# Softmax maxima by 32x32 block transposes and one TensorE transpose, in a two-layer cross-attention kernel

## Chip, cores and metric

The kernel runs on one core of a Trainium2 chip. The metric is the device time of one execution in microseconds (us); where several executions were timed, their median is used. All arithmetic is float32. The engines are TensorE (PE; its weight loads are shown apart as PEld), VectorE (DVE), ScalarE (ACT), GpSimd (POOL) and SyncE (SP, which issues most DMAs).

## What is computed

Two cross-attention layers, one after the other, on x of 4 batches x 512 tokens x 320 channels, with a context of 4 x 1024 tokens x 512. There are 20 heads of 16 channels. The last 4 context tokens are "ip" tokens in layer 0; in layer 1 the first 77 are text and all others ip. Cut to what matters (`heads` splits the channels):

```python
# layer 0
q, k_t, v_t = heads(x @ W_q), heads(text @ W_k), heads(text @ W_v)
probs_t = softmax(q . k_t * 0.25)                 # over 1020 text tokens
text_out = probs_t @ v_t
attn_scores = q . heads(ip @ W_k_ip) * 0.25       # 4 ip tokens
qsem = l2norm(probs_t @ text);  sem = qsem . l2norm(ip)
probs_ip = softmax(attn_scores + 0.5 * sem) * spatial_mask
x = (text_out + probs_ip @ heads(ip @ W_v_ip)) @ W_out + b_out + x
# layer 1
out = softmax(q . k * 0.25) @ v                   # over 77 text tokens
    + softmax(q . k_ip * 0.25) @ v_ip             # over 947 ip tokens
x = out @ Wo.T + bo + x
```

Each softmax subtracts the maximum over its own tokens, per query and head.

## The kernel before, in words

**Tiling.** The queries come in 16 turns: 4 batches of 4 tiles of 128 tokens (`TURNS`, line 34). A turn has 5 groups of 4 heads (`HG`), so there are 80 groups of layer 0 (`G`, line 491) and 80 of layer 1. Layer 1 of a turn can begin when layer 0 of that turn is finished, so its groups run beside the layer-0 groups of later turns: 75 of them as objects of class `Once` (line 557), the last turn's 5 by another routine (`twice`, line 696).

**Scores.** `fill` (line 510) makes the scores of one group for half of the context tokens. Four heads lie in four 32-row strips of the `kq` and `qq` tiles, 16 rows used in each. Scores have the context tokens on the partitions and (head, token block, query) along the free axis: two PSUM tiles `sc` of 128x1024. ScalarE copies each to SBUF (`e`, line 523), VectorE reduces each over the token blocks into `m` (line 525); after the second half the two halves of `m` are combined (line 528).

**Maxima.** What is left is a maximum over 128 partitions, for 4 heads x 128 queries. TensorE transposes `m` head by head (four transposes of 128x128, `max0`, line 835; in layer 1 another four of the first token block, where text and ip meet, `maxima`, line 572). VectorE reduces the transposes out of PSUM into `zz` (four or eight columns, line 847 and lines 584 to 587), turns `zz` by one 32x32 block transpose and SyncE writes it to DRAM in four DMAs (`spread`, line 531). Broadcast DMAs bring it back to all partitions as `bc`. VectorE adds `bc` to `e`, and ScalarE takes the exponential in place (lines 597 to 604 for layer 1, 854 to 863 for layer 0; GpSimd subtracts one head's exponentials from the other's at line 865).

**The ip tokens of layer 0** are the last four partitions of the last token block. Lines 824 to 826 put `drop` (-1e30 on these partitions) into `m`, line 861 puts it into the exponent, and lines 828 to 830 copy the four score rows to a tile `ips`, which `finish` transposes at line 1023.

**Products of layer 0.** A group has two units (class `Unit`, line 903) of two heads. A unit has seven products of eight matmul records each, in four parts: `11`, `12` (part 0), `t1` and `s2`x`t2` (part 1), `22` and `t3` (part 2), `t4` (part 3). Their results lie in two PSUM banks, and VectorE or ScalarE must read a bank (`c`, `p`, `u`, `pv` in the trace) before it is written anew; `t1` writes the bank that product `12` used, so it waits for `c` and `pv` of part 0. GpSimd adds into `e` between products (lines 933, 952, 955).

**Values of layer 1.** `add_values` (line 538) multiplies the exponentials with the values into `pv`; ScalarE copies it to `pc`. In `normalise` (line 657) VectorE spreads the denominators over 32 partitions by a shuffle and takes their reciprocal over 128x256; GpSimd multiplies and adds text and ip. `project` (line 668) multiplies the five groups with `wo1`.

**Order.** All instructions of TensorE, and those of VectorE that go through `vec`, keep the order of the program (lines 76 to 92). The order is written out by hand: after each part k = 0 to 7 of a group (4 per unit), `stop` (line 1155) runs one step of waiting work. Even stops `visit`: the fills of the next layer-0 group at k = 0 and 2, those of a layer-1 group at k = 4 and 6, the `pv` products of the one before at 6. Odd stops take steps of finishing a turn (`after`, `late`) and of the projections (`proj`) of the next batch, which are used up in the first 12 or so of a batch's 20 groups; the last batch has none to prepare. Exponentials follow at k = 1 and 6 (layer 0, `ew`), 3 and 5 (layer 1, `do_adds`), `normalise` at 1 (at 5 in a turn's first group). The transposes of the maxima stand in part 0, between products `11` and `12` (line 953): of layer 1 in a group's first unit, of layer 0 in its second. Behind the last group the remaining work of layer 1 follows in a loop (line 1215).

## Time and profile before

| | us |
|---|---|
| median of 3 runs | 3419.3 (3416.9 to 3419.7) |
| the profiled execution | 3412.7 |
| its span, first to last instruction | 3411.0 |
| TensorE busy | 3302.7 |
| VectorE busy | 2486.3 |
| ScalarE busy | 1787.4 |
| GpSimd busy | 1036.4 |
| transposes `mx` of the maxima, 920 | 141.4 |
| reductions `zz` out of PSUM, 305 | 168.0 |
| shuffle and reciprocal of layer 1's denominators, 80 each | 175.3 |

The profile is of one execution. Busy time of an engine is the time in which at least one of its instructions runs; matmuls overlap, so the time between the starts of two of them says more than a record's duration. A float32 product stands as two records, a transpose as one. In the timeline each line has start, duration, engine, line of the program (L77 is the helper for matmuls, L92 that for transposes, L87 that for VectorE), the operation, out<-in by the program's names, and in brackets how long the engine was idle before and what ended that.

### The profile page before, as it was taken

How to read it: one execution, taken by the hardware profiler on the slowest of the kernel's cores; microseconds unless marked ns; L12 is line 12 of the kernel's file. 1: busy time of each engine (PE TensorE's matmuls, PEld its weight loads, DVE VectorE, ACT ScalarE, POOL GpSimd, SP SyncE). 2: the span in 40 equal slices, each digit the busy share in tenths (PEclk: the TensorE clock that was granted, in tenths of full speed). 3: DMA queues.
4: the chain of work that ended last, by engine and by line, in shares of the span. 5: the costliest groups of instructions: out<-in, count | busy, mean ns of one | idle time of the engine just before them, and what ended most of it. 6: DMA issues, size and time to landing. Idle time of an engine off the chain costs nothing.

```text
span 3411.0 us, 74812 instructions
## 1 busy us (share of the span) xinstructions
PE 3302.7 (97%) x28417; PEld 2666.0 (78%) x28417; DVE 2486.3 (73%) x4300; ACT 1787.4 (52%) x3220; POOL 1036.4 (30%) x1066
## 2 busy tenths in 40 slices
PE   7999999999999999999999999999999999999978
PEld 6777887878778888887878788787877878787855
DVE  2344676688877766788886776778888888888864
ACT  1344455555555555555555555556555655565642
POOL 2323223233233222333333222223333333333220
PEclk9999999999999999999999999999999999999986
DMA  7423444333434444332345444332242332232221
GB/s 211 103 58 99 103 112 102 91 67 66 102 93 118 101 110 120 69 67 57 71 97 131 103 100 110 88 71 60 63 100 65 64 61 64 58 67 60 59 52 34
DMA packets 644271, 292.23 MB, mean 86 GB/s; under 512 B 491162, under 2 KB 598394, under 8 KB 643914
## 3 DMA queue, kind: packets, MB, share of 16 engines
q1 hardware_dynamic: 642874, 283.83, 35.1%
q8 instruction: 228, 3.74, 0.5%
q0 software_dynamic: 864, 3.41, 0.4%
q14 instruction: 129, 1.06, 0.1%
q10 hardware_dynamic: 176, 0.20, 0.0%
HBM read 245.95 MB, written 40.63 MB: 84 GB/s over the span
## 4 chain that ended last, share of the span: by engine, by line
PE 83%; DVE 10%; DMA 2%; ACT 2%; issue 2%; SPq 1%; POOL 0%; DVEq 0%; POOLq 0%; ACTq 0%
PE b L77 53%; PE sc L77 9%; PE pt_k L77 4%; PE pv L77 4%; PE pt_v L77 4%; DVE e L87 4%; PE mx L92 3%; DVE m L87 2%; PE pt_q L77 2%; PE pt_y L77 1%; DVE den L87 1%; ACT e L523 1%; PE ex L77 1%; PE mx L77 1%; ACT e L604 1%
## 5 line engine op out<-in xcount | busy, mean ns | idle before, releaser
L87 DVE TENSOR_REDUCE m<-sc 128x256 f32<-128x1024 f32 (+1 forms) x620 | 662.2, 1084 | 163.6 <-PE sc L77 119.8
L87 DVE TENSOR_TENSOR e<-e,bc 128x768 f32<-128x768 f32 (+2 forms) x770 | 751.4, 1024 | 14.0 <-DMA bc<-zd 14.0
L77 PE MATMUL b<-xv_t,e 128*128 128x277 f32 x2560 | 685.2, 409 | 21.8 <-DVE pv L87 15.0
L77 PE MATMUL b<-xv,e 128*128 128x277 f32 x2560 | 652.7, 397 | 8.6 <-ACT e L863 8.6
L523 ACT COPY e<-sc 128x1024 f32<-128x1024 f32 x620 | 613.2, 1009 | 70.0 <-DVE m L87 39.3
L77 PEld LDWEIGHTS b<-xv_t,e 128*128 128x128 f32 x2560 | 460.3, 189 | 150.1 <-issue 10.3
L77 PEld LDWEIGHTS b<-xv,e 128*128 128x128 f32 x2560 | 470.3, 190 | 111.5 <-ACT e L863 10.7
L865 POOL TENSOR_TENSOR e<-e 128x512 f32<-128x512 f32 x160 | 206.8, 1292 | 1059.0 <-ACT e L863 1059.0
L937 ACT ACTIVATE junk<-c 128x256 f32<-128x256 f32 x480 | 198.6, 414 | 523.5 <-DVE c L87 520.5
L604 ACT ACTIVATE e<-e 128x1024 f32<-128x1024 f32 x300 | 312.5, 1057 | 238.5 <-DVE e L87 232.8
L952 POOL TENSOR_TENSOR e<-e,s 128x512 f32<-128x512 f32 x160 | 211.8, 1324 | 578.6 <-PE b L77 554.4
L77 PEld LDWEIGHTS sc<-qq,kq 16*128 16x128 f32 x9920 | 306.2, 186 | 102.3 <-issue 96.2
L863 ACT ACTIVATE e<-e 128x1024 f32<-128x1024 f32 x320 | 337.4, 1057 | 59.3 <-DVE e L87 50.0
L77 PE MATMUL sc<-qq,kq 16*128 16x128 f32 x9920 | 365.7, 283 | 2.0 <-DMA kq<-kd 1.1
L87 DVE TENSOR_TENSOR c<-b,p 128x256 f32<-128x256 f32 x320 | 134.5, 420 | 312.3 <-PE b L77 303.8
L77 PE MATMUL b<-xs,e 128*128 128x256 f32 x1280 | 304.6, 381 | 0.0
L77 PE MATMUL b<-xs_t,s 128*128 128x256 f32 x1280 | 302.9, 379 | 0.0
L77 PE MATMUL b<-xs_t,e 128*128 128x256 f32 x1280 | 302.4, 379 | 0.0
L77 PEld LDWEIGHTS b<-xs_t,s 128*128 128x128 f32 x1280 | 243.3, 190 | 39.7
L77 PEld LDWEIGHTS b<-xs_t,e 128*128 128x128 f32 x1280 | 243.2, 190 | 33.1
L77 PEld LDWEIGHTS b<-xs,e 128*128 128x128 f32 x1280 | 239.2, 190 | 36.3 <-issue 2.0
L955 POOL TENSOR_TENSOR e<-e,s 128x512 f32<-128x512 f32 x160 | 206.3, 1290 | 186.1 <-PE b L77 185.8
(201 smaller groups left out, 3634.3 us busy)
## 6 DMA issues: line engine op xcount, KB each, us to landing
kq<-kd SPq DMA_DIRECT2D x632, 64.0 KB
bc<-zd SPq DMA_DIRECT2D x155, 256.0 KB
v1q<-v1d SPq DMA_DIRECT2D x80, 373.5 KB
xv<-v0d SPq DMA_DIRECT2D x320, 42.0 KB
xv_t<-v0d SPq DMA_DIRECT2D x320, 42.0 KB
bc<-zd SPq DMA_DIRECT2D x75, 154.0 KB
L_xattn_W_k<-in_L_xattn_W_k_dram SPq DMA_DIRECT2D x13, 640.0 KB
L_xattn_Wv_ip<-in_L_xattn_Wv_ip_dram SPq DMA_DIRECT2D x13, 640.0 KB
```

Of the source, the lines that this page charges most:

```text
L77: tc.keep_in_program_order(nc.tensor.matmul(out, lhsT=lhsT, rhs=rhs, start=start, stop=stop, skip_group_check=on))
L87: return lambda *args, **kw: keep(getattr(self.engine, name)(*args, **kw))
L92: tc.keep_in_program_order(nc.tensor.transpose(out, in_, ident))
L523: nc.scalar.copy(e[i].rearrange("p h t s -> p (h t s)"), ps[i].rearrange("p h n -> p (h n)"))
L604: nc.scalar.activation(flat, flat, AF.Exp)
L863: nc.scalar.activation(flat, flat, AF.Exp)
L865: nc.gpsimd.tensor_tensor(e[:, 1], e[:, 1], e[:, 0], ALU.subtract)
L937: nc.scalar.activation(junk, x, AF.Square, accum_out=self.w["ss"][:, self.h + r, k : k + 1])
L952: nc.gpsimd.tensor_tensor(self.e("11"), self.e("11"), self.s2, ALU.add)
L955: nc.gpsimd.tensor_tensor(self.e("12"), self.e("12"), self.s2, ALU.subtract)
```

## The change

The maxima are first folded on VectorE: a block transpose turns every 32x32 block of the 128x512 maxima, a reduction over the inner 32 leaves 16 columns (4 heads x 4 blocks of queries) per softmax in `zz`, and one TensorE transpose of `zz` brings the four partition blocks side by side; a last reduction on VectorE takes the maximum over these four, with the sign turned. `spread` writes that in one DMA. In layer 1, which has two softmaxes, ScalarE adds a mask column (`cut`) to the first token block when the first half is filled, and the fold has two block transposes, two additions with the other mask column, and a reduction of both at once. The folds stand at the stops k = 3 (layer 0) and 7 (layer 1), and the transposes move behind product `12`.

The ip mask of layer 0 becomes a 17th row of keys (-1e30 on the last four tokens) against a 17th row of ones in the queries, so that the scores come out masked, the second half's reduction runs over all four blocks, and `drop` goes. The ip scores, which the masked scores no longer hold, are computed in `finish` from the queries and the ip keys (`kip`, spread by heads with a mask `ownk`).

In layer 1's `normalise`, a block transpose of `pc` puts the denominators into one column, so that the reciprocal has 8 numbers per partition; pairs of groups are packed and turned back by a block transpose (`turn_back`), and the projection has three products for five.

```diff
-    zz = [cst.tile([P, ZW], F32, name=f"zz{l}") for l in range(2)]
+    zz = cst.tile([P, P], F32, name="zz")
...
+    nc.vector.memset(qq[0][0], 1.0)
+    nc.vector.memset(kq[0][0], 0.0)
+    for r in range(4):
+        rows = kq[0][0][32 * r : 32 * r + 32, T - NIP :]
+        nc.gpsimd.affine_select(out=rows, in_=rows, compare_op=ALU.not_equal, fill=NEVER, base=-D,
+                                pattern=[[0, NIP]], channel_multiplier=1)
...
+                kip = st2.tile([P, NC, NIP], F32, tag="kip", name=f"kip_{b}")
+                nc.gpsimd.memset(kip, 0.0)
+                for c, (c0, m) in enumerate(CK):
+                    nc.sync.dma_start(kip[:m, c, :], z.kd[0][c0 : c0 + m, T - NIP :])
+                z.kip = st2.tile([P, NC, H, NIP], F32, tag="kipd", name=f"kipd_{b}")
+                nc.gpsimd.tensor_tensor(z.kip, kip.unsqueeze(2).to_broadcast([P, NC, H, NIP]), ownk, ALU.mult)
...
+        n = D + 1 - l
...
-        lo, hi = (1 - c, TH) if l else (0, TH - c)
+        lo = l * (1 - c)
...
-                              ps[j][:, :, lo * P : hi * P].rearrange("p h (t s) -> p h s t", s=P), AX.X, ALU.max)
+                              ps[j][:, :, lo * P : TH * P].rearrange("p h (t s) -> p h s t", s=P), AX.X, ALU.max)
         if c:
-            vec.tensor_tensor(m[:, 0], m[:, 0], m[:, 1], ALU.max)
+            vec.tensor_tensor(m[:, l], m[:, 0], m[:, 1], ALU.max)
+        elif l:
+            for i in range(2):
+                nc.scalar.activation(m[:, 2, 2 * i : 2 * i + 2, :], e[i][:, :, 0, :], AF.Identity, bias=cut[:, 0:1])
...
+    def blocks(m, o, i):
+        vec.transpose(m[:, o].rearrange("p h s -> p (h s)"), m[:, i].rearrange("p h s -> p (h s)"))
+
+    def turn_tops(name):
+        pt = tp(f"mx{name}")
+        tr(pt[:, 0:P], zz, ident)
+        return pt
+
+    def spread(pt, rows, tag, name):
+        n = rows * P // ZW
+        zt = st2.tile([ZW, ZW], F32, tag="zt", name=f"zt{name}")
+        vec.tensor_reduce(zt[:n, :], pt[:n, 0:P].rearrange("r (b j) -> r j b", j=ZW), AX.X, ALU.max, negate=True)
         zd = dr.tile([rows, P], F32, tag=tag, name=f"{tag}{name}")
-        for k in range(P // ZW):
-            nc.sync.dma_start(zd[:, ZW * k : ZW * (k + 1)], zt[ZW * k : ZW * k + rows, :])
+        nc.sync.dma_start(zd.rearrange("h (k j) -> (h k) j", j=ZW), zt[:n, :])
...
+        def fold(self):
+            m = self.m
+            self.folded = True
+            blocks(m, 0, 2)
+            for i in range(2):
+                x = m[:, 1, 2 * i : 2 * i + 2, :]
+                vec.scalar_tensor_tensor(x, self.e[0][i][:, :, 0, :], cut[:, 1:2], x, ALU.add, ALU.max)
+            blocks(m, 2, 1)
+            vec.tensor_reduce(zz[:, 0:ZW].rearrange("p (w r) -> p w r", w=2),
+                              m[:, 0:3:2].rearrange("p w h (k j) -> p w (h k) j", j=ZW), AX.X, ALU.max)
...
-            d = big.tile([P, 2 * P], F32, tag="den", name=f"den1_{turn}_{g}")
-            vec.stream_shuffle(d, pc, [D] * 32)
-            vec.reciprocal(d, d)
-            nc.gpsimd.tensor_tensor(d, pc, d, ALU.mult)
-            nc.gpsimd.tensor_tensor(box["o"][:, g, :], d[:, 0:P], d[:, P:], ALU.add)
+            d = big.tile([P, 8, ZW], F32, tag="den", name=f"den1_{turn}_{g}")
+            r = big.tile([P, 8], F32, tag="rden", name=f"rden1_{turn}_{g}")
+            vec.transpose(d.rearrange("p k w -> p (k w)"), pc)
+            vec.reciprocal(r, d[:, :, D])
+            if g % 2 == 0:
+                if g:
+                    turn_back(g // 2 - 1)
...
+            lo = D * (g % 2)
+            nc.gpsimd.tensor_tensor(d[:, :, 0:D], d[:, :, 0:D], r.unsqueeze(2).to_broadcast([P, 8, D]), ALU.mult)
+            nc.gpsimd.tensor_tensor(box["t"][:, :, lo : lo + D], d[:, 0:4, 0:D], d[:, 4:8, 0:D], ALU.add)
...
-            for g in range(HG):
-                mm(pt[:, 0:C], box["o"][:, g, :], wo1[:, g, :], g == 0, g == HG - 1)
+            for n in range(NO):
+                mm(pt[:, 0:C], box["o"][:, n, :], wo1[:, n, :], n == 0, n == NO - 1)
...
-            for i in range(2):
-                x = m[:, 0, 2 * i : 2 * i + 2, :]
-                vec.scalar_tensor_tensor(x, e[i][:, :, TH - 1, :], drop[:, 0:1], x, ALU.add, ALU.max)
-            turn, g = G[gi]
-            for i in range(2):
-                row = (2 * g + i) * NIP
-                nc.sync.dma_start(of(turn)["ips"][row : row + NIP], e[i][P - NIP :, :, TH - 1, :])
...
+    def fold0(gi):
+        if gi < len(G):
+            m = ms.pop(gi)
+            blocks(m, 1, 0)
+            vec.tensor_reduce(zz[:, 0 : ZW // 2], m[:, 1].rearrange("p h (k j) -> p (h k) j", j=ZW), AX.X, ALU.max)
...
-            if c == 0:
-                (vec.tensor_tensor(e, e, mine.unsqueeze(2).to_broadcast([P, 2, TH, P]), ALU.add))
-            else:
...
-                (vec.scalar_tensor_tensor(y, y, drop[:, 0:1], mine, ALU.add, ALU.add))
+            vec.tensor_tensor(e, e, mine.unsqueeze(2).to_broadcast([P, 2, TH, P]), ALU.add)
...
-            reduce = between()
             self.product(self.b2, "12", "21", True)
             nc.gpsimd.tensor_tensor(self.e("12"), self.e("12"), self.s2, ALU.subtract)
-            if reduce and not self.i:
-                reduce()
+            ask = between()
             self.add_square(self.b2[:, 0:EH], self.p1[:, 0:EH], 0, 0)
             vec.tensor_tensor(self.values(0), self.b2[:, EH:], self.p1[:, EH:], ALU.add)
-            if reduce and self.i:
-                reduce()
+            if ask:
+                ask()
...
+        qt = zero_below(big.tile([P, NC, P], F32, tag="xT1", name=f"q0t_{turn}"))
+        for c, (c0, n) in enumerate(CK):
+            nc.sync.dma_start(qt[:n, c, :], z.q0d[c0 : c0 + n, s * P : (s + 1) * P])
...
-            for k in range(2):
-                tr(pt.rearrange("p (q k n) -> p k q n", k=2, n=NIP)[:, k], ips[:, k, :], ident[: NP * NIP, : NP * NIP])
+            for c in range(NC):
+                mm(pt, qt[:, c, :], z.kip[:, c].rearrange("p h n -> p (h n)"), c == 0, c == NC - 1)
...
+        if k == 3:
+            fold0(gi + 1) if gi + 1 < len(G) else do_fold()
+        if k == 7:
+            do_fold()
         if k % 2:
             item(after, late)
             item(proj)
```

## The prediction

> **What bounds the kernel now.** I read four views: the page's busy shares and slices, the groups of instructions by line, the timeline of one period late in the run, and who waited for whom. The page first:

> ```profile
> PE 3302.7 (97%) x28417; PEld 2666.0 (78%) x28417; DVE 2486.3 (73%) x4300; ACT 1787.4 (52%) x3220; POOL 1036.4 (30%) x1066
> ...
> PE   7999999999999999999999999999999999999978
> ...
> DVE  2344676688877766788886776778888888888864
> ```

> TensorE leaves 3% idle, so an instruction taken from it should shorten the run by its issue time. But VectorE stands at eight tenths in most later slices, and every added step here is VectorE's. Whether the gain survives is decided where TensorE waits for VectorE, so next comes that place, in the timeline: the end of one layer-1 group, from its second score fill (`sc`) to the next fill.

> ```profile
> 2662.12 1.17 PE L77 MATMUL sc<-qq,kq 16*128 16x128 f32 x32
> ...
> 2663.22 2.14 PE L77 MATMUL b<-xv_t,e 128*128 128x277 f32 x8
> 2663.43 1.22 DVE L87 TENSOR_REDUCE m<-sc 128x256 f32<-128x1024 f32 x1 [0.49 <-PE sc L77]
> ...
> 2664.97 1.23 DVE L87 TENSOR_REDUCE m<-sc 128x256 f32<-128x1024 f32 x1 [0.31 <-ACT e L523]
> 2665.20 2.03 PE L77 MATMUL b<-xv,e 128*128 128x277 f32 x8
> ...
> 2666.83 0.17 DVE L87 TENSOR_TENSOR pv<-b,p 128x21 f32<-128x21 f32 x1
> 2667.07 0.60 PE L92 MATMUL mx<-ident,e 128*128 128x128 f32 x4
> ...
> 2667.38 1.27 POOL L952 TENSOR_TENSOR e<-e,s 128x512 f32<-128x512 f32 x1 [1.91 <-PE b L77]
> 2667.51 0.60 PE L92 MATMUL mx<-ident,m 128*128 128x128 f32 x4
> 2667.70 1.35 DVE L87 TENSOR_REDUCE zz<-mx 128x4 f32<-128x308 f32 x3 [0.70 <-PE mx L92]
> 2667.94 2.04 PE L77 MATMUL b<-xv,e 128*128 128x277 f32 x8
> ...
> 2669.91 1.17 PE L77 MATMUL sc<-qq,kq 16*128 16x128 f32 x32
> ```

> Columns: start, duration, engine. TensorE never pauses; its eight transposes (`mx`) sit between the products `11` and `12`, and VectorE has had `m` ready since 2666.9. The last pair of lines comes from another place of the timeline and shows what VectorE meets when GpSimd is adding:

> ```profile
> 2745.59 1.28 POOL L865 TENSOR_TENSOR e<-e 128x512 f32<-128x512 f32 x1 [6.19 <-ACT e L863]
> 2745.60 1.37 DVE L87 TENSOR_TENSOR sem<-pv,rn 128x80 f32<-128x80 f32 x1
> ```

> An 80-column operation that takes 0.24 us alone (the shortest of its 16) lasted until GpSimd's add was over.

> **What TensorE sheds.** Start-to-start, transposes of 128 columns follow each other every 0.109 us. Layer 1 falls from eight to one: 0.76 us, times 75 groups in that form, 57 us. Layer 0 falls from four to one: 0.33 us times 80, 26 us. The output projection of layer 1 multiplies three packed pairs instead of five groups; a float32 product is two records, so 10 records become 6 at 0.269 us start-to-start: 1.08 us times 16 turns, 17 us. Against that the ip scores become a product: six records of 80 columns for two transposes of 40. Weight loads bound such short ones (4-column products of `pt_k` follow every 0.112 us), so 0.67 less 0.17 us, times 16: 8 us added. Sum: 92 us off TensorE. The 17th row lies in the same 32-row strip as the other 16, and 32 records of `sc` still take 1.10 us; the nearest row, `ex` with 19 rows in the tail, goes two strips at a time at a lower clock and bounds it only loosely: 0.08 us a record against 0.034. I take zero.

> **What VectorE gains and loses, off the critical stretches.** Normalising a layer-1 group sheds shuffle 0.44 and reciprocal 1.75 us; it gets a transpose of 256 columns (0.44, as the shuffle), a reciprocal of 8 numbers (0.28, from 20 columns) and three 128-column transposes per five groups (about 0.2 each group): 1.3 us less, 80 times. In most periods this falls where VectorE then idles for the next fill, so it is worth nothing; in the second period of a turn the exponentials were late behind it and the `pv` products stood 0.2 and 0.71 us (2767.51, 2770.04). I credit 0.9 us in 12 turns, 10 us. The layer-0 additions of the second half become one operation (1.22 for 0.95 and 0.48): idle time too. ScalarE gets two 128x256 activations per layer-1 group, some 0.8 us, beside the 1.59 us that it idles before copying `u`; without that cover the product on `b1` would slip by the excess. GpSimd's multiply and add halve. SyncE issues one DMA for four behind the maxima and drops two `ips` copies per group; three `q0t` loads a turn and three key loads a batch come instead. All of these stand in front of window loads that wait for TensorE anyway, and the matmuls hardly wait for any DMA now (`kq`: 1.1 us in all). The new memsets and selects run once, in the first slice where VectorE is at two tenths: zero.

> **The fold in layer 0.** In the stretch from 2679.37 the two reductions grow by 0.27 us each, the two additions of `drop` (0.88) go, and a 512-column transpose and a reduction 512 to 16 come. The reduction is 0.68 (`zz<-mx` of 512 columns). The transpose at this width is in no row: 32 columns take 0.212, a shuffle of 256 takes 0.44, a reduction of 512 takes 0.68. The shuffle's slope gives 0.71; below, nothing is faster than 0.53 (512 numbers at the slope of these rows); above, twice the slope, 1.24. I take 0.71, the shuffle being the nearest kind. Then `zz` is ready at 2684.5, and TensorE comes for it behind product `12` at 2685.2: no wait. The additions of line 604 that follow start later, but they no longer sit under GpSimd's add at line 952 (they took 2.35 us for two, 1.4 alone), so `c` and `pv` are done by 2686.4, just when TensorE needs their bank. The 26 us stand.

> **The fold in layer 1** is the costly one. After `pv`, from 2666.92: transpose to 2667.63; two scalar_tensor_tensor of 256 columns, 0.48 each, both inputs in SBUF; transpose 0.71; reduction of 1024, 1.22. But line 952 starts at 2667.38, and nearly every two-SBUF-input operation of some length that starts under a GpSimd add lasts until its end (768 columns of `e<-e,bc`: 0.95 alone, median 1.82 under it; the 32-column transpose and the reductions are the same either way). So the pair ends about 2669.4, the transpose 2670.13, the reduction 2671.4, and with 0.2 us of handing over TensorE transposes at 2671.6. It has been ready since product `12`, now at 2667.17, ended at 2669.05: a wait of 2.55 us, behind which the next fill and every later product queue. On VectorE `c`, `pv` and then the last reduction (of the transposed maxima, 0.25) follow the fold, and behind that the reductions of the next fill, which wait for this fill anyway.

> What covers the wait is a step of projection or normalisation that TensorE does between the fill and product `11`. From the timeline, the stretch from fill to fill lasts 6.7 us (no step) in 31 of the 74 groups in the main loop, 6.9 to 7.5 (a few transposes) in 19, and over 8 in 24. The bare ones wait 2.55 us (25 times), 1.7 in the 6 at a turn's end (where `t1` now stands 1.16 us for `pv`, less 0.3), the middle ones some 2.2 us, the others not: 64 + 10 + 42 = 116 us.

> [...]

> **Sum.** -92 - 10 + 116 = +14 us. The tail behind 3260 us loses five reciprocals and gains folds in front of late additions; I take zero, 5 either way. The profiled execution took 3412.7 us (span 3411.0 and 1.7 around it), 6.6 under the median of the runs shown; put on that median, 3419.3 + 14 = 3433.

> **Rivals.**
> Faster, by one mechanism: the pair in layer 1's fold is not held by line 952. It would have to get through before 2667.4, or the two engines not exclude each other here. Then each of some 48 waits is 0.95 us shorter, -45: 3388. For it: the margin at the start is 0.2 us. Against it: with the first of the pair ahead, the second still meets the add, as the additions at 2683.40 show; it decides only if both are done before.
> Fully hidden: TensorE finds `zz` ready everywhere. Then 92 and 10 come off: 3317. This needs the fold 2.5 us shorter, against the chain above.
> Slower transposes, or new waits: at 1.24 us the second transpose adds 0.53 to 48 waits, and layer 0's `c` comes late by as much some 30 times: +40, 3473; with ScalarE's two activations pushing `u` late as well, up to 3500. For it: no row has this width.
> That the change doesn't do what it says: the transposes go in any case, the diff has one where eight stood.

> **Numbers.** Forecast case 0.52 (3415 to 3455, by counting 10 middle waits more or less and the handing over); held pair absent 0.18; hidden 0.08; slower transposes and waits 0.22. The range reaches from 3385 to 3485 and leaves out the hidden case and the worst of the last. A measurement of this kernel can tell about 0.2%, 7 us, from no change. Faster by more than that: 0.18 + 0.08 and 0.01 of the forecast case, 0.27. Within: 0.14 of the forecast case. Slower: 0.59. The signs are mixed; the forecast case alone is 3415 to 3455.

> **What would show it.** `mx` with 155 records; `pt_y<-wo,o` with 96; waits of "PE mx for DVE zz" of about 100 us in all, some 50 long ones near 2.5 us, in the half of the run without projections, and next to none in layer 0; scalar_tensor_tensor `m<-e,cut,m` well above 0.48 us in the mean; the 512-column transpose near 0.71. The prediction is wrong if those waits are short (then 3390 or less), if `b` waits for `pv` or `c` in layer 0, or if the pair runs at 0.48.

## The result and the profile after

The changed kernel takes 3507.9 us (median of 4 runs, 3505.2 to 3513.1) where the kernel before took 3418.1 (4 runs, 3415.9 to 3419.7): a ratio of 1.0265, interval 1.0247 to 1.0283. It is 90 us slower; the forecast was 14 us slower, and the range ended at 3485. The profiled execution took 3505.7 us, with a span of 3503.6 and a mean granted TensorE clock of 0.959 (before: 0.984).

The page of the changed kernel, busy shares and two rows of slices:

```profile
PE 3299.4 (94%) x27652; PEld 2648.1 (76%) x27652; DVE 2528.2 (72%) x4104; ACT 1859.3 (53%) x3370; POOL 1013.9 (29%) x1114
...
PE   7999999999999999999999999999999999999978
...
DVE  2344677778867777788877777778788878887864
```

TensorE is busy as long as before, though 765 records are gone. Idle time is only part of the answer. The timeline of one layer-1 fold (start, duration, engine; shortened to VectorE's chain and TensorE's next steps):

```profile
2641.75 0.17 DVE L88 TENSOR_TENSOR pv<-b,p 128x21 f32<-128x21 f32 x1
2641.86 0.71 DVE L88 STREAM_TRANSPOSE m<-m 128x512 f32<-128x512 f32 x1
...
2642.36 1.27 POOL L987 TENSOR_TENSOR e<-e,s 128x512 f32<-128x512 f32 x1 [1.07 <-PE b L78]
2642.50 1.81 DVE L88 SCALAR_TENSOR_TENSOR m<-e,cut,m 128x256 f32<-128x256 f32 x2
...
2644.34 0.71 DVE L88 STREAM_TRANSPOSE m<-m 128x512 f32<-128x512 f32 x1
2645.09 1.22 DVE L88 TENSOR_REDUCE zz<-m 128x32 f32<-128x1024 f32 x1
...
2646.36 0.33 PE L93 MATMUL mx<-ident,zz 128*128 128x128 f32 x1 [2.25 <-DVE zz L88]
...
2646.62 1.45 PE L78 MATMUL sc<-qq,kq 17*128 17x128 f32 x32
...
2648.01 3.49 PE L78 MATMUL b<-xv_t,e 128*128 128x277 f32 x8
```

The fold runs as the prediction wrote it down: 0.71 for the transpose, the pair held by GpSimd's add, 1.22 for the reduction, and TensorE waits 2.25 us. What it did not write down stands in the last two lines: the fill takes 1.45 us in place of 1.17, and the eight records behind it 3.49 in place of 2.14. The stretches view of the same place, four windows of 3.41 us (PE busy first; the number ahead of the DMA share is the granted clock):

```profile
2640.54:2643.96 3.42, 3.42 (x16) 2.45 (x14) 3.39 (x6) 1.26 (x6) 2.02 (x2) 1.00 0.31 55
2643.96:2647.37 3.41, 1.16 (x26) 0.89 (x29) 2.98 (x6) 0.51 (x2) 1.27 (x1) 1.00 0.15 21
2647.37:2650.78 3.41, 3.41 (x22) 2.56 (x17) 2.35 (x2) 2.02 (x2) 0.00 (x0) 0.50 0.04 11
2650.78:2654.20 3.42, 3.42 (x22) 3.06 (x22) 2.67 (x4) 0.94 (x2) 0.00 (x0) 1.00 0.65 160
```

In the second window TensorE idles 2.25 us at full clock; in the third it never idles, and its clock is granted at one half. The pause is followed by a second loss, half of 3.41 us, and that time counts as busy. The waits of TensorE (us in total, times, longest):

```profile
PE mx L93 <- DVE zz L88: 124.2, 57, 4.1
PE b L78 <- DVE zt L88: 18.2, 29, 2.8
```

For every kernel below, the span is split in three from its trace: **idle** (no record of TensorE runs, between its first record and its last), **half** (half the length of the stretches whose granted clock is 0.50, that is what they cost), and the rest, **work** at full clock (with some 9 us ahead of the first record and behind the last, in every kernel). Medians carry 4 to 10 runs; ratios are to the runs of the kernel before on the same chip.

| kernel | median | ratio, 95% interval | span | work | idle | half |
|---|---|---|---|---|---|---|
| before | 3418.1 | | 3411.0 | 3257.9 | 98.7 | 54.4 |
| after | 3507.9 | 1.0265 [1.0247, 1.0283] | 3503.6 | 3162.7 | 194.9 | 146.0 |
| e1 pair first | 3414.0 | 0.9983 [0.9969, 0.9996] | 3414.1 | 3167.8 | 149.5 | 96.8 |
| e2 filler, four | 3446.6 | 1.0082 [1.0063, 1.0100] | 3444.6 | 3262.4 | 104.3 | 77.9 |
| e12 filler, three | 3449.3 | 1.0102 [1.0083, 1.0121] | 3453.0 | 3235.1 | 128.2 | 89.7 |
| e5 filler, two | 3465.0 | 1.0140 [1.0125, 1.0155] | 3462.5 | 3215.2 | 147.4 | 99.9 |
| e3 early fold | 3431.2 | 1.0033 [1.0020, 1.0046] | 3425.6 | 3167.0 | 163.7 | 94.9 |
| e6 early, k = 6 | 3471.7 | 1.0168 [1.0148, 1.0188] | 3465.7 | 3167.0 | 190.2 | 108.5 |
| e9 late top | 3417.9 | 0.9998 [0.9988, 1.0008] | 3416.6 | 3157.5 | 164.5 | 94.6 |
| e11 top in part 1 | 3317.9 | 0.9717 [0.9700, 0.9734] | 3312.7 | 3160.1 | 95.3 | 57.3 |
| e7 normalisation only | 3373.9 | 0.9872 [0.9858, 0.9887] | 3370.6 | 3236.2 | 78.7 | 55.7 |
| e8 + 17th row | 3362.2 | 0.9841 [0.9826, 0.9855] | 3360.4 | 3235.4 | 70.7 | 54.3 |
| e10 + fold of layer 0 | 3355.8 | 0.9814 [0.9799, 0.9828] | 3354.5 | 3209.6 | 84.2 | 60.7 |
| e4 layer 1 as before | 3357.6 | 0.9819 [0.9802, 0.9835] | 3359.8 | 3213.1 | 77.5 | 69.2 |

From before to after, work falls by 95.2 us (forecast 92), idle time grows by 96.2 (forecast: 116 of waits less a credit of 10), and half grows by 91.6 (forecast: nothing). The split can be trusted to some 10 us: six kernels of the table (after, e1, e3, e6, e9, e11) have the same 27652 TensorE records, and their work lies between 3157.5 and 3167.8 us while their spans differ by up to 191.

### The profile page after: what moved, and what is told of

It reads as the page before. It is cut to its first block, busy times and chain, and to the rows that moved or that the text cites. A ratio compares the mean times of both kernels' runs of the same rounds, so it can differ in the third digit from the quotient of the medians.

```text
span 3503.6 us, 72387 instructions
## 1 busy us (share of the span) xinstructions
PE 3299.4 (94%) x27652; PEld 2648.1 (76%) x27652; DVE 2528.2 (72%) x4104; ACT 1859.3 (53%) x3370; POOL 1013.9 (29%) x1114
## 2 busy tenths in 40 slices
PE   7999999999999999999999999999999999999978
## 3 DMA queue, kind: packets, MB, share of 16 engines
q0 software_dynamic: 864, 3.41, 0.3%
## 4 chain that ended last, share of the span: by engine, by line
PE 71%; DVE 19%; ACT 6%; issue 2%; DMA 2%; SPq 0%; POOL 0%; DVEq 0%; ACTq 0%; POOLq 0%
PE b L78 47%; DVE m L88 10%; PE sc L78 8%; PE pt_k L78 4%; PE pt_v L78 4%; DVE e L88 4%; ACT e L898 3%; DVE zz L88 2%; PE pt_q L78 2%; PE pv L78 2%; ACT e L544 1%; PE pt_y L78 1%; DVE c L88 1%; PE mx L93 1%; PE mx L78 1%
## 5 line engine op out<-in xcount | busy, mean ns | idle before, releaser
L88 DVE TENSOR_REDUCE m<-sc 128x256 f32<-128x1024 f32 (+1 forms) x620 | 704.1, 1157 | 230.7 <-PE sc L78 175.3
L88 DVE TENSOR_TENSOR e<-e,bc 128x1024 f32<-128x1024 f32 (+2 forms) x770 | 768.6, 1047 | 6.5 <-DMA bc<-zd 6.5
L78 PE MATMUL b<-xv_t,e 128*128 128x277 f32 x2560 | 748.9, 439 | 24.4 <-DVE zt L88 18.2
L78 PE MATMUL b<-xv,e 128*128 128x277 f32 x2560 | 631.6, 398 | 8.9 <-DVE pv L88 6.0
L78 PEld LDWEIGHTS b<-xv_t,e 128*128 128x128 f32 x2560 | 498.0, 205 | 173.0 <-issue 29.4
L987 POOL TENSOR_TENSOR e<-e,s 128x512 f32<-128x512 f32 x160 | 208.9, 1306 | 604.8 <-PE b L78 591.1
L78 PE MATMUL sc<-qq,kq 17*128 17x128 f32 (+1 forms) x9920 | 377.2, 289 | 1.9 <-DMA kq<-kd 1.6
L78 PEld LDWEIGHTS sc<-qq,kq 17*128 17x128 f32 (+1 forms) x9920 | 315.4, 191 | 83.3 <-issue 75.3
L78 PE MATMUL b<-xs_t,s 128*128 128x256 f32 x1280 | 312.2, 388 | 0.0
L78 PEld LDWEIGHTS b<-xs_t,s 128*128 128x128 f32 x1280 | 254.0, 198 | 46.3
L989 POOL TENSOR_TENSOR e<-e,s 128x512 f32<-128x512 f32 x160 | 219.9, 1374 | 84.8 <-PE b L78 83.0
```

The lines of the kernel that those rows point to most:

```text
L78: tc.keep_in_program_order(nc.tensor.matmul(out, lhsT=lhsT, rhs=rhs, start=start, stop=stop, skip_group_check=on))
L88: return lambda *args, **kw: keep(getattr(self.engine, name)(*args, **kw))
L987: nc.gpsimd.tensor_tensor(self.e("11"), self.e("11"), self.s2, ALU.add)
L989: nc.gpsimd.tensor_tensor(self.e("12"), self.e("12"), self.s2, ALU.subtract)
```

## The experiments

The theory: a pause of about 2.2 us costs its own length and then half the clock for one or two windows of 3.41 us. The rivals: the clock falls for another reason (load), or in proportion to idle time without a threshold.

**e1: order in the fold.**

```diff
-            blocks(m, 0, 2)
             for i in range(2):
                 x = m[:, 1, 2 * i : 2 * i + 2, :]
                 vec.scalar_tensor_tensor(x, self.e[0][i][:, :, 0, :], cut[:, 1:2], x, ALU.add, ALU.max)
+            blocks(m, 0, 2)
             blocks(m, 2, 1)
```

> The changed kernel with one change of order: in layer 1's fold the two scalar_tensor_tensor stand ahead of the first block transpose, so that they start before GpSimd's add of L987 does; the instructions are the same. Clock theory (a pause of about 2.2 us at mx costs its own length, and then half the clock for 3.4 to 6.8 us): the pair takes 0.9 us in place of 1.8, the pauses fall to about 1.3 us, TensorE's idle time from 195 to some 150 us, and since no 3.41-us window with less than 1.4 us of idle time was followed by half clock, the time lost to it falls from 146 to some 65 us: about 3380 to 3400 us. Rival, pauses cost their own length alone and the clock is low for another reason (power, the denser stream): only the 45 us of idle time go, half-clock time stays near 146 us: about 3463 us. Rival, the pair is held in any order: 3508 us.

The pair took 0.88 us, the usual pause fell to 1.31, idle time by 45.4 us, as all but the last rival had it. The time fell by twice that, since half fell by 49.2. But half fell to 97, not 65, and the time missed the expected range by 14 us: the bound of 1.4 us that I had read from the trace of the change was too high. It did not even hold there: a window with 1.23 us of idle time, at 3146 us, is followed by half clock. In e1, of 30 windows with 1.2 to 1.4 us of idle time, 16 were.

**e2, e12, e5: dummy work in the pause.** Four, three or two products that nothing reads, in groups where no projection is left:

```diff
     def turn_tops(name, fillers=0):
         pt = tp(f"mx{name}")
+        for _ in range(fillers):
+            mm(pt[:, 192:512], ident, bo[0], True, True)
         tr(pt[:, 0:P], zz, ident)
...
-            self.folded = True
+            self.folded, self.bare = True, not proj
...
-            pt = turn_tops(self.name)
+            pt = turn_tops(self.name, 4 if self.bare else 0)
```

> The changed kernel with more work and nothing less: four dummy products (128x128 by 128x320, 8 records of about 0.27 us, written to columns of the mx bank that nothing reads) stand ahead of the transpose mx in layer-1 groups that have no projection step left, so that TensorE is busy in the time in which it waited for zz. Clock theory: the pauses shrink from 2.2 to some 0.2 us, half-clock time falls from 146 to some 70 us, and the run gets faster by doing more: 3430 to 3445 us. Rival, the half clock comes from load (power) or has no relation to the pauses: half-clock time stays or grows, and the time is 3508 us or above. Rival, the added records themselves delay the stream where no wait was: up to 3530 us.

> The changed kernel with two dummy products of 128x320 (4 records, about 1.08 us) in place of the four of e2_filler, at the same places. Dummy work and remaining wait together are as long as the wait of the changed kernel, so by idle and work alone nothing changes: a theory that counts only busy and idle time of TensorE says 3508 us. Clock theory: the pauses fall from 2.2 to 1.1 us; in the six kernels seen, 64 windows of 3.41 us held over 1.95 us of idle time, 63 of them followed by half clock; of 5230 windows with under 1.2 us, one was. Then half-clock time falls from 146 to 75 to 90 us with idle and work unchanged in sum: 3435 to 3450 us, the same as with four. Rival, the clock follows idle time in proportion, without a threshold: half of the effect of e2_filler, some 110 us of half clock, 3470 us.

> The third dose: three dummy products of 128x320 where e5_fill_half has two and e2_filler four, so that the pauses in bare periods become about 0.6 us; about ten pauses of 1.9 to 2.3 us elsewhere stay in all three. Half-clock time was 146 us with pauses of 2.2, 100 with 1.15, 78 with 0.1. If half clock follows idle time in proportion, 0.6 us give about 90 us and, as dummy work and idle time make up the same sum, 3453 us. If there is a band from 1.0 to 1.95 us of idle time per window of 3.41 us in which it comes in part, and nothing below (one window in 11300 so far), half-clock time is that of e2, 72 to 82 us, and the time 3434 to 3446 us.

With four, 100 us of work were added and the run got 61 us faster. The timeline of e2 at such a place:

```profile
2658.05 2.31 PE L78 MATMUL mx<-bo,ident 128*128 128x320 f32 x8
...
2660.44 0.33 PE L93 MATMUL mx<-ident,zz 128*128 128x128 f32 x1
...
2660.69 1.20 PE L78 MATMUL sc<-qq,kq 17*128 17x128 f32 x32
...
2661.82 2.14 PE L78 MATMUL b<-xv_t,e 128*128 128x277 f32 x8
```

Fill and product take 1.20 and 2.14 us again, at full clock. The time, 3446.6 us, lies 1.6 above the expected range. Load as the cause is out: more load, less half clock. Work and idle time together are 3357.6 us in the changed kernel and 3362.6 to 3366.7 in these three, so their gain is clock and nothing else: half is 146, 100, 90 and 78 us for usual pauses of 2.2, 1.15, 0.6 and 0.1 us. But e5 and e12 missed their expected times by 15 and 3 us, with half 10 and 8 us above what I expected of a threshold, and both come close to the sums for proportion (3470 and 3453). The windows decide between the two. This is the count over all fourteen kernels of the table, for the windows of 3.41 us that begin between 100 and 3250 us at full clock:

| idle time in the window, us | windows | followed by half clock |
|---|---|---|
| under 0.5 | 11847 | 1 |
| 0.5 to 1.0 | 362 | 0 |
| 1.0 to 1.2 | 96 | 9 |
| 1.2 to 1.4 | 89 | 22 |
| 1.4 to 1.95 | 117 | 57 |
| over 1.95 | 134 | 132 |

In e12 alone 52 windows had 0.5 to 1.0 us, and none was followed; its 17 stretches before 3250 us all follow windows with over 1.4, from pauses that have no filler. Of such windows, 17 of 18 were followed in e12 and 14 of 17 in e2: 5 of the 12 us of half that e12 has above e2 are these three stretches, and the other 7 lie ahead of 100 and behind 3250 us. So it is a band, not proportion: below 1 us once in some 12200 windows, nearly always above 1.95. What decides inside the band stays open. The window shown above, ahead of half clock, was not idle throughout: TensorE was busy in it for 1.16 us.

**e3 and e6: begin the fold earlier.** The text half of the fold (known after the first fill) is done ahead of the rest, at k = 5 in e3, at k = 6 ahead of layer 0's additions in e6:

```diff
+        def prefold(self):
+            m = self.m
+            for i in range(2):
+                x = m[:, 0, 2 * i : 2 * i + 2, :]
+                vec.scalar_tensor_tensor(x, self.e[0][i][:, :, 0, :], cut[:, 1:2], x, ALU.add, ALU.max)
+            blocks(m, 1, 2)
+            vec.tensor_reduce(zz[:, 0:16], m[:, 1].rearrange("p h (k j) -> p (h k) j", j=ZW), AX.X, ALU.max)
```

> The changed kernel with layer 1's fold begun earlier: at the stop k = 5 (k = 1 in the last group) the scalar_tensor_tensor pair, the block transpose of the text maxima (now known after the first half) and a reduction of 512; at k = 7 only one block transpose and a reduction of 512. Same amount of work, one reduction of 1024 is now two of 512. Clock theory: the fold behind the second fill takes 1.4 us where it took 4.6, so TensorE finds zz ready or waits under 0.8 us; idle time near 110 us, half-clock time near 60 us; the full gain of TensorE's shed work (95 us) shows: 3320 to 3365 us. Rival, clock independent of pauses: only the 100 us of waits go, half-clock time stays at 146: about 3410 us. Rival, the work moved to k = 5 delays c, pv or the exponentials there and the waits come back at b: 3430 to 3500 us.

> As e3_early_fold (the text half of layer 1's fold, with the scalar_tensor_tensor pair, ahead of the rest), but one stop later: at k = 6, behind c of the second unit's products and ahead of the layer-0 additions and the second fill, where no bank of the products waits for VectorE. From the timeline of e1_pair_first VectorE idles 1.2 us (0.33, 0.63, 0.25) between there and the fold; the moved 2.3 us use these up and push the reductions by 1.1, the fold behind them is 2.1 us shorter. Expected: the waits of b for pv of e3 (87 us) go, waits at mx about 0.3 us in a bare period; idle 95 to 110 us, half-clock time 65 to 75 us, work 3167 us: 3330 to 3350 us. Rival, the late reductions push the copies of sc and the exponentials of layer 0, and the waits come back at b or sc: 3380 to 3430 us.

Both missed; the third case of e3 and the rival of e6 came, e6 beyond it (3472 against 3380 to 3430). The waits at `mx` went (4.3 and 5.8 us left) and came back as "b for DVE pv": 86.8 and 115.0 us. The timeline of e6:

```profile
2729.85 1.26 POOL L991 TENSOR_TENSOR e<-e,s 128x512 f32<-128x512 f32 x1
...
2730.41 1.25 DVE L88 TENSOR_TENSOR m<-m 128x512 f32<-128x512 f32 x1
2731.58 0.17 DVE L88 TENSOR_TENSOR pv<-b,p 128x21 f32<-128x21 f32 x1
...
2731.80 3.81 PE L78 MATMUL b<-xv,e 128*128 128x277 f32 x8 [2.39 <-DVE pv L88]
```

I had looked for idle time of VectorE and found 1.2 us, but not for the first operation behind it that TensorE waits for: `pv`, 0.17 us long, which in e1 was done 0.2 us before product `12` needed its bank. Pushed later, the two-input maximum ahead of it also fell under GpSimd's add (1.25 in place of 0.69). A pause of 2.39 us, and the records behind it at half clock again.

**e9 and e11: fetch `zz` later.** The fold keeps its place, with the pair first as in e1, but TensorE comes for `zz` later; the transposes go into the tile that will hold `bc`. In e9 the reduction stands in part 1, the TensorE transpose and the last reduction in part 2; e11 moves them to part 0 and part 1 (`top(2)` runs the reduction, `top(1)` the rest). The first line below is in both, the rest is e11 against e9:

```diff
+            now["top"].extend([self.reduce, lambda: self.ask(turn_tops(self.name))])
...
             if ask:
                 ask()
+            top(2)
...
             vec.tensor_tensor(self.p5[:, EH:], self.b3[:, EH:], self.p1[:, EH:], ALU.subtract)
-            top(2)
+            top(1)
...
             self.add_square(self.b3[:, 0:EH], self.u, 0, 1)
-            top(1)
```

> The changed kernel with the same folds, but TensorE no longer comes for zz right behind product 12: at k = 7 VectorE does the scalar_tensor_tensor pair and the two block transposes of layer 1 (into the tile that bc will fill later), the reduction of 1024 to zz stands behind the copies p of part 1, the TensorE transpose behind the first product of part 2, and the last reduction behind c there; the broadcast is some 7 us later, where the additions that need it come 14 us after the old place. Work is that of the changed kernel (3163 us at full clock). Clock theory with the order as the cause: the 120 us of waits at mx go and nothing takes their place, half clock is left at the ends only: idle 75 to 95, half-clock time 55 to 75 us: 3295 to 3335 us, better than both kernels and than e4. Rival, VectorE has no room anywhere: the same 4.4 us of fold push p, c or pv and the waits come back at b, as in e3 and e6: 3400 to 3470 us. Rival, the later broadcast is late for the additions: waits of pv for e, 3350 to 3400 us.

> As e9_late_top, but earlier: the reduction of 1024 directly behind c and pv of part 0, the TensorE transpose between t1 and the second product of part 1, and the last reduction behind the copies p. In e9 the broadcast landed 0.7 and 1.0 us too late for the additions at k = 3, and c, pv and t1 behind these waited 1.6 us in each bare period; nothing else waited. Here it leaves 3.6 us earlier, and ahead of the next key loads. From e9's timeline, p then ends 2711.3 to 2711.6 where the product that needs its bank starts at 2711.8. Expected: no wait of more than 0.3 us in a bare period, idle 80 to 100 us, half-clock time 55 to 75 us, work 3163 us: 3300 to 3340 us, the fastest of all. Rival, p is late and the waits come at the product on its bank (c or pv as releaser): 3360 to 3400 us.

In e9 the third case came, worse than its range (3418 against 3350 to 3400; the number lies in the second case's range, the waits are those of the third). Its timeline from the second fill of layer 1 to k = 3 of the next group:

```profile
2715.42 1.17 PE L78 MATMUL sc<-qq,kq 17*128 17x128 f32 x32
2715.49 0.32 SPq L570 DMA_DIRECT2D zd<-zt  x1
...
2722.01 0.43 DVE L88 TENSOR_TENSOR e<-e,bc 128x256 f32<-128x256 f32 x1 [0.72 <-DMA bc<-zd]
...
2723.46 1.11 DVE L88 TENSOR_TENSOR e<-e,bc 128x768 f32<-128x768 f32 x1 [1.03 <-DMA bc<-zd]
...
2725.25 2.11 PE L78 MATMUL b<-xv_t,e 128*128 128x277 f32 x8 [1.63 <-DVE zt L88]
```

The broadcast landed late, in the stretch of the next group's key loads (whether these delayed it was not tried), and `t1` waited behind the additions. Against the next fill, e11 sends the maxima (`zd<-zt`) 3.8 us earlier. VectorE's additions waited for the broadcast as follows (us in total, times, longest), in e9 (first line) and in e11:

```profile
DVE e L88 <- DMA bc<-zd: 104.0, 109, 4.3
DVE e L88 <- DMA bc<-zd: 8.0, 4, 3.2
```

In e11 TensorE pauses at `mx` only twice in the whole run, 5.6 us in all (timeline, a fold's second half):

```profile
2634.91 1.21 DVE L88 TENSOR_REDUCE zz<-bc 128x32 f32<-128x1024 f32 x1
...
2635.41 2.14 PE L78 MATMUL b<-xv_t,e 128*128 128x277 f32 x8
...
2636.03 2.34 DVE L88 TENSOR_REDUCE m<-sc 128x256 f32<-128x1024 f32 x2
...
2637.38 0.27 PE L93 MATMUL mx<-ident,zz 128*128 128x128 f32 x1
...
2637.49 1.89 PE L78 MATMUL b<-xs_t,s 128*128 128x256 f32 x8
...
2639.01 0.32 SPq L570 DMA_DIRECT2D zd<-zt  x1
...
2642.77 1.17 PE L78 MATMUL sc<-qq,kq 17*128 17x128 f32 x32
```

The reduction and the fold's hand-over lie beside `t1`, and the time is 3317.9 us, 2.8% under the kernel before, with the work of the changed kernel. Time, idle and half all lie in the expected ranges.

**e4, e7, e8, e10: parts of the change alone.** e7 is the kernel before with the new `normalise`, `turn_back` and `project`; e8 adds the 17th row and the ip product; e10 adds layer 0's fold; e4 is e10 with layer 1's eight transposes moved behind product `12`. In e4, as against the change:

```diff
-            pt = turn_tops(self.name)
-            return lambda: self.ask(pt)
+            first, rest = [tp(f"mx{self.name}_{k}").rearrange("p (h t) -> p h t", h=4) for k in range(2)]
+            for h in range(4):
+                tr(first[:, h, :], self.e[0][h // 2][:, h % 2, 0, :], ident)
+            for h in range(4):
+                tr(rest[:, h, :], self.m[:, 0, h, :], ident)
+            return lambda: self.ask(first, rest)
```

> The changed kernel with the maxima of layer 1 as in the kernel before (eight TensorE transposes, reductions out of PSUM; no fold at k = 7, no activations with the mask), while layer 0's fold, the 17th row and the packed normalisation stay. If all the harm lies in layer 1's fold, its 57 us of transposes come back and every long wait at mx goes, with the half clock behind it: idle near 95 us, half-clock time near 55 us, and the 26 + 17 + 10 - 8 us of the other parts remain as a gain: about 3373 us. Rival, layer 0's fold or the ip product also cost: 3400 us or more. Rival, the half clock comes from the rest of the change: half-clock time stays near 146 us and the time near 3460 us.

> The kernel before with the new normalisation and packed projection alone (denominators by block transposes, three products for five); maxima and mask as before. The prediction's terms: 17 us of TensorE work less and 10 us of waits in the second period of a turn, 27 us: about 3390 us. Rival from e4_layer 1 as before, which was some 14 us faster than the terms of the other parts add up to: the shorter reciprocals also shorten the end of the run, behind 3250 us, where idle time fell from 48 to 29 us: about 3375 us. Rival, hidden: 17 us alone, 3400 us.

> The kernel before with the new normalisation and the 17th row with the ip product; the maxima of both layers as before (4 and 8 TensorE transposes, at their old place). Against e7_norm_only this shows the 17th row and the ip product alone, against e4_l1_as_before layer 0's fold alone. The prediction's terms: 17th row nothing, ip product 8 us slower, layer 0's fold 26 us faster than its old transposes: about 8 us above e7_norm_only and 26 us above e4_l1_as_before, some 3384 to 3398 us. Rival, 17 rows cost more than 16 or the q0t loads are waited for: 15 us or more above e7_norm_only. Rival, dropping the two additions of the mask and the ips copies from VectorE and SyncE pays: below e7_norm_only.

> e8_old_maxima with layer 0's fold alone in place of its four transposes (17th row, ip product and new normalisation in both; layer 1's maxima and their place as before). e4_l1_as_before had the same fold, but also moved layer 1's eight transposes behind product 12, and was only 5 us faster than e8, with 22 us less work of TensorE, 7 more idle and 15 more at half clock, at pauses of 2.1 to 2.8 us at a batch's or turn's end. If the moved layer-1 transposes made these pauses: about 22 to 26 us below e8, 3336 to 3342 us. Rival, layer 0's fold itself makes them (fold and additions late in the last periods of a turn): as e4, about 3357 us.

e7 met its first rival (3375), e8 its second (below e7), e4 was better than any case, and e10 met its rival: layer 0's fold saves 25.8 us of work and gives most of it back. Where, the timeline of e10 at the start of a batch's projections shows:

```profile
1263.90 1.27 POOL L991 TENSOR_TENSOR e<-e,s 128x512 f32<-128x512 f32 x1 [0.69 <-PE b L78]
1263.98 1.47 DVE L88 TENSOR_TENSOR sums<-raw 128x256 f32<-128x256 f32 x1
...
1265.89 1.49 DVE L88 SCALAR_TENSOR_TENSOR sums<-raw,last 128x256 f32<-128x256 f32 x1
...
1269.33 0.27 DVE L88 TENSOR_REDUCE zt<-mx 16x32 f32<-16x128 f32 x1
...
1269.66 1.72 PE L78 MATMUL b<-xv_t,e 128*128 128x277 f32 x3 [2.82 <-DVE zt L88]
```

The fold pushes four `sums` operations back, so that two of them are held by GpSimd's adds (1.47 and 1.49 us, where the other two take 0.48 and 0.47); `c` and `pv` come late behind them, and `t1` waits 2.82 us; the first three records behind that wait take 1.72 us, as at half clock (eight take 2.14 at full clock, at 1259.30). TensorE's idle time ahead of this product grows from 17.1 us in e8 to 30.7: three such places, two of 1.5 us, and many of 0.16. That is all of the 13.5 us of idle time; half clock adds 6.4.

## Why the prediction was wrong

The direction was right, the size was not. Spans, as the parts are added one by one (before, e7, e8, e10, after), against the prediction's terms:

| part | forecast | measured | work | idle | half |
|---|---|---|---|---|---|
| normalisation, projection | -27 | -40.4 | -21.7 | -20.0 | +1.3 |
| 17th row, ip product | +8 | -10.2 | -0.8 | -8.0 | -1.4 |
| fold of layer 0 | -26 | -5.9 | -25.8 | +13.5 | +6.4 |
| fold of layer 1 | -57 + 116 | +149.1 | -46.9 | +110.7 | +85.3 |
| sum | +14 | +92.6 | -95.2 | +96.2 | +91.6 |

- **The step that failed: "64 + 10 + 42 = 116 us" as the price of the waits.** It counted each wait once. The waits were there nearly as written (110.7 us of idle time for 116; at `mx` 57 of them, the usual one 2.2 us where 2.55 was forecast); what they did to the granted clock cost another 85 us, which the sum had at nothing. e2 shows it by removing the pauses and not their time. The trace of before held the hint: between 100 and 3250 us it has two half-clock stretches, each behind a window with over 1.2 us of idle time. The changed kernel has 39, and half in that part is 83.6 us against 3.4.
- **The fold in layer 1**: right in its mechanism. The 512-column transpose took 0.711 us (taken: 0.71, from the shuffle), the pair 0.80 each on average, 0.48 in e1 with the order turned. The rival "pair not held" put 45 us on that, and idle time fell by 45.4; the clock made it 94 in the median. One reading behind the pair's price was low: the 26 additions of 768 columns that start under a GpSimd add of 512 columns in the trace of before take 2.02 us in the median, not 1.82; the sum does not use it.
- **"The 26 us stand", "no wait" in layer 0**: the work came out at 25.8, in part by luck: from e8 to e10 the transposes themselves give 20.1 us (35.1 less for 320 gone, 15.0 more for 80 new ones), the rest lies in other records. The absence of waits was wrong. Cover was looked for in one bare period; at the batch starts the `sums` operations stand in the same place.
- **What TensorE sheds**: 92 forecast, 95.2 measured. The projection's records fell from 44.2 to 27.2 us start-to-start, 17.0 as forecast. Layer 1's fold gave 47 in place of 57; a lone transpose takes 0.19 us to the next start (15.0 us for 80 in e10), not the 0.109 of one in a row, which is about half of these 10 us. What the rest is stays open.
- **The credit of 10 us** for normalisation was too small: idle time fell by 20.0.
- **The ip product** costs nearly what was forecast (10.0 us for its 96 records, 10.7 forecast; the two transposes that it replaces cost 3.9), yet the part gains: idle time fell by 8.0 without the two mask additions and the `ips` copies, and work did not rise, since other records stood closer together (`b<-xv,e` 4.8 us less). Which of these did it was not tried alone. 17 rows cost the same as 16 (283 ns a record for both in e8).
- **The rival "fully hidden", 3317 us, against "the chain above"**: e11 took 3317.9, with 97.8 us less work (92 forecast) and 3.4 less idle time (10 forecast), so that the closeness of the two numbers is in part luck. The chain was right for its place; that TensorE must fetch `zz` right behind product `12` was taken for given.

## What to carry to other kernels

Price a pause of the bounding engine by what follows it too: read the granted clock in the window behind the pauses that the trace already has, and prefer pauses under 1 us, each in a window of its own, to one over 2 (here 1 of 12209 windows with under 1 us of idle time was followed by half clock, and 132 of 134 with over 1.95). When a serial chain appears on a nearly full engine, don't only ask where that engine idles, but which short operation behind the new work another engine waits for; here the consumer could fetch later at no cost (e11), though not as late as in e9, where the producer could not be earlier (e3, e6). And a change of several parts is worth taking apart: in the order in which they were added, three of these four gain (40, 10 and 6 us, the last little more than the noise), and the one that loses gains in another place.
